# Splitting the second half's projection weights at fixed places in an attention loop

## The chip, the cores and the metric

The kernel runs on one core of a Trainium2 chip. A core has a matmul engine (TensorE, in the profile PE, with its weight loads as PEld), three engines for elementwise work (VectorE or DVE, ScalarE or ACT, GpSimd or POOL) and SyncE (SP), whose queue here issues every DMA. The metric is the device time of one execution in microseconds; lower is better. The kernel before takes 2299.53 us, the median of 2297.73, 2299.53 and 2301.41.

## The reference

One layer: causal linear attention with rotary positions over 4096 tokens of width 512 (16 query heads, 4 key/value heads, 128 wide), then a layer norm and a gated feed-forward part with Hadamard transforms. The change touches only the attention part:

```python
x: (1, 4096, 512)
q = (x @ Wq.T)   # 16 heads of 128
k = (x @ Wk.T)   # 4 heads of 128
v = (x @ Wv.T)   # 4 heads of 128
q = q * cos + rotate_half(q) * sin
k = k * cos + rotate_half(k) * sin
# each key/value head serves 4 query heads
qf = elu(q) + 1
kf = elu(k) + 1
# over tokens s, per head:
state = state + kf_s[:, None] * v_s[None, :]
z = z + kf_s
out_s = (qf_s @ state) / (qf_s @ z + EPS)
# then
out @ Wo.T
```

## The kernel before

**Products.** Every fp32 factor is held as two tiles, a rounded `hi` and the rest `lo`, and every product takes three matmuls (hi by hi, hi by lo, lo by hi). The pair is made by `hilo` (lines 94 to 99): ScalarE copies the source to `hi` (line 95) and VectorE or GpSimd, by its argument `eng`, subtracts to `lo` (line 96). A weight tile is 128x512. It is read from HBM into a *raw* tile and split from there into two tiles, `wh` and `wl`. Raw tiles come from the pool `praw`, with three buffers (line 64). The split weights live in the pool `wres`, with 28 buffers (line 63): 24 for the twelve tiles of one pass, and four more.

**Two passes, blocks and slots.** Attention runs in two passes over the tokens, s = 0 and s = 1, with half of the heads each: 8 query heads and 2 key/value heads, so that each pass needs twelve weight tiles of its own: two of v, two of k (one per key/value head g) and eight of q (four per g). A pass has 16 blocks of 256 tokens; blocks 16 to 31 are pass 1. A block has four *slots* `(n, g, p)`: a key/value head g and half p of the block's tokens (two chunks of 64). The loop over the 128 slots begins at line 534; slot i belongs to block i // 4, and pass 1 starts at slot 64.

**What a slot does.** `scores` forms the scores of two chunks (matmuls at lines 380 and 381, evacuation by ACT at 387, sums on DVE at 390 and 391, causal selects on POOL at 394). `av` multiplies scores and states into `ps_num` (line 414), which ACT empties at 418; `ps_num` has two PSUM buffers. `state` forms the chunks' states (337 to 354). Ahead of these go the projections for later slots: the q projection `proj_q(i + 5)` runs five slots ahead of its use (24 matmuls at line 288 into `ps_qk`, rotary steps at 268 to 278), `proj_k` and `proj_v` of the next block once per block (`proj_v` starts in slot (0, 1) with 24 matmuls at line 241 into `ps_v`, and sends its result through the DMAs `vs` and `vd`). `ps_qk` and `ps_v` share three PSUM buffers. So pass 1's v weights are first used in slot 61, its k weights in slot 60, and its q weights from slot 59 on, each with pass 0's work still going on.

**Weights of pass 1.** They go into the buffers that the same tiles of pass 0 and the spare four leave. In the loop's program `weights_v` and `weights_k` (198 to 203) stand at slot 54 (r = -6), `weights_q` (204 to 207) for the first key/value head at slot 56 (r = -4) and for the second at slot 58 (r = -2). Each loads a raw tile and splits it; the subtraction is on VectorE, for the odd q heads on GpSimd.

**The spare buffers.** `wcomb` (427 to 441) sums weights of the later feed-forward part on GpSimd, a step per slot: four tiles `wsum` of the pool `wres` are read, summed and stored to `was_d` in DRAM. It runs in slots 4 to 51 and 62 to 109.

**Order.** The program is traced in the order in which Python runs it, and a scheduler then orders each engine's queue (SP's DMA issues included) by readiness in its own model. An instruction that is *pinned* (`keep_in_program_order`, through `pin` and the argument of `dma`) keeps its place behind everything traced before it on its engine. The weight loads above are not pinned. Tiles of pools carry the dependencies: a tile's new writer waits until the old contents have been read.

Of the kernel before, what the change touches and what calls it, by code (L numbers as in the profile page):

```python
# [9 lines left out]
F32 = mybir.dt.float32  # L10
F32R = mybir.dt.float32r
# [12 lines left out]
QA = 5  # L24
# [19 lines left out]
def kernel(  # L44
# [6 lines left out]
    V, S, G, T = nc.vector, nc.scalar, nc.gpsimd, nc.tensor  # L51

    def dma(dst, src, pin=False):
        if dst.dtype == F32R:
            dst = dst.bitcast(F32)
        if src.dtype == F32R:
            src = src.bitcast(F32)
        i = nc.sync.dma_start(dst, src)
        if pin:
            tc.keep_in_program_order(i)  # L60

    cpool = ctx.enter_context(tc.tile_pool(name="cpool", bufs=1))
    wres = ctx.enter_context(tc.tile_pool(name="wres", bufs=28))
    praw = ctx.enter_context(tc.tile_pool(name="praw", bufs=3))
# [20 lines left out]
    def pin(i):  # L85
        tc.keep_in_program_order(i)
# [7 lines left out]
    def hilo(hi, lo, src, eng=V, pinned=False):  # L94
        i = S.activation(hi, src, AF.Copy)  # L95
        j = eng.tensor_tensor(lo, src, hi.bitcast(F32), ALU.subtract)  # L96
        if pinned:
            pin(i)
            pin(j)

    def load_w(src, pool=wres, eng=V, raw=None, **kw):
        raw = load_raw(src) if raw is None else raw
        hi, lo = (pool.tile([128, 512], F32R, tag="w", name=n, **kw) for n in ("wh", "wl"))
        hilo(hi, lo, raw, eng)
        return hi, lo

    WO = {}
    RAW0 = {}
# [3 lines left out]
    def wo_raw(h, raw):  # L112
        WR[h] = raw
        dma(raw, wo[h], True)
# [64 lines left out]
    with ExitStack() as es:  # L179
# [15 lines left out]
        W = {}  # L195
        blk = {}

        def weights_v(s, j):
            W["v", s, j] = load_w(wv[s, :, j * 512:(j + 1) * 512], raw=RAW0.pop(("v", s, j), None))

        def weights_k(s, g):
            W["k", s, g] = load_w(wk[2 * s + g], raw=RAW0.pop(("k", s, g), None))

        def weights_q(s, g):
            for h in range(4):
                W["q", s, g, h] = load_w(wq[8 * s + 4 * g + h], raw=RAW0.pop(("q", s, g, h), None),
                                         eng=G if h % 2 else V)
# [220 lines left out]
        def wcomb(p):  # L428
            r = {}
            for it in range(2):  # L430
                for kh in range(2):
                    x = wres.tile([128, 2, 2, 128], F32, tag="w", name="wsum")
                    dma(x, wug[2 * p + it].rearrange("p (u k m) -> p u k m", u=2, k=4)[:, :, 2 * kh:2 * kh + 2], True)
                    r[it, kh] = x
            yield
            yield
            for key, o, a, b, op in (("S3", (0, 0), (0, 0), (1, 0), ALU.subtract), ("S1", (1, 0), (1, 0), (1, 1), ALU.add),
                                     ("S2", (1, 1), (0, 0), (1, 1), ALU.subtract), ("S4", (0, 1), (0, 1), (1, 1), ALU.add)):
                pin(G.tensor_tensor(r[o], r[a], r[b], op))
                yield  # L440
                yield
                dma(was_d[p][key], r[o].rearrange("p u k m -> p (u k m)"), True)

        def wcomb_all():
            for p in range(8):
                yield from wcomb(p)
                yield
                yield
# [3 lines left out]
        def o_load(g, hi, lo):  # L452
            if g < 2:
                nt = praw.tile([128, 512], F32, tag="raw", name="nt0")
                dma(nt, num_d[0][:, g], True)
                rb = praw.tile([128, 512], F32, tag="raw", name="rb0")
                dma(rb, rec_d[0][g * 512:(g + 1) * 512].partition_broadcast(128), True)
            else:
                nt = ntx[:, g]
                dma(nt, num_d[0][:, g], True)  # L460
                pre_rb(g)
                rb = RB.pop(g)
            O0[g] = (hi, lo, nt, rb)

        def o_mul(g):
            pin(G.tensor_tensor(O0[g][3], O0[g][2], O0[g][3], ALU.mult))

        def o_split(g, eng):
            hi, lo, nt, rb = O0[g]
            hilo(hi, lo, rb.rearrange("p (h n) -> p h n", h=4), eng, True)  # L470
            cur.setdefault(0, {})[g] = (hi, lo)
# [32 lines left out]
        def go(gen):  # L504
            if gen is not None:
                next(gen, None)

        def run(gen):
            for _ in gen:
                pass  # L510
# [18 lines left out]
        for j in range(SA):  # L529
            run(scores(j))  # L530
        nsc = SA
        gw = wcomb_all()
        gk = gs1 = gv = None
        for i, (n, g, p) in enumerate(slots):
            nxt = n + 1 < N
            sl = (g, p)
            r = i - 4 * (NB - 1)
            if r == -6:
                for j in range(2):
                    weights_v(1, j)  # L540
                    weights_k(1, j)
            if r == 1 - QA:
                weights_q(1, 0)
            if r == 3 - QA:
                weights_q(1, 1)
            go(gq)
            if sl == (0, 1):
                go(gk)
# [44 lines left out]
            for x in gsc:  # L593
                go(x)
            gq = gq2
            if 4 <= i < 52 or 62 <= i < 110:
                go(gw)
            elif i == 113:
                o_load(0, *(wres.tile([128, 4, 128], F32R, tag="w", name=x) for x in ("oh0", "ol0")))
            elif i == 114:  # L600
                o_mul(0)
            elif i == 115:
                o_split(0, G)
                o_load(1, *(wres.tile([128, 4, 128], F32R, tag="w", name=x) for x in ("oh0", "ol0")))
            elif i == 116:
                o_mul(1)
            elif i == 117:
                o_split(1, G)
            elif i == 118:
                for h in range(3):  # L610
                    wo_raw(h, praw.tile([128, 512], F32, tag="raw", name="woraw"))
            elif i == 119:
                for x in ("xh", "xl"):
                    x = pe.tile([128, 4, 256], F32, tag=x, name="woraw").rearrange("p a b -> p (a b)")
                    wo_raw(len(WR), x[:, 0:512])
                    wo_raw(len(WR), x[:, 512:1024])
            elif i == 121:
                wo_split(G, 0, 1)
                wo_split(V, 2)
                for h in range(7, 10):  # L620
                    wo_raw(h, praw.tile([128, 512], F32, tag="raw", name="woraw"))
            elif i == 122:
                wo_split(G, 3, 4)
                wo_split(V, 5)
                o2 = [p3.tile([128, 2, 4, 128], F32R, tag=t, name=t, bufs=4) for t in ("qh", "ql")]
            elif i == 123:
                wo_split(G, 6)
                early.close()
                late["s"] = ExitStack()
                late["p"] = late["s"].enter_context(tc.tile_pool(name="cl", bufs=2, side="right", reuse_waits="tile"))  # L630
                ntx = late["p"].tile([128, 4, 512], F32, tag="nt", name="ntx", bufs=2)
                for y in range(2):
                    o_load(2 + y, o2[0][:, y], o2[1][:, y])
                x = p2.tile([128, 4, 512], F32, tag="vd", name="woraw")
                for h in range(10, 14):
                    wo_raw(h, x[:, h - 10])
                for h in range(14, 16):
                    wo_raw(h, ntx[:, h - 14])
                pre_rb(4)
                pre_yp(0)  # L640
                pre(1)
            elif i == 124:
                wo_split(G, 7)
                wo_split(V, 8)
            elif i == 125:
                o_mul(2)
                wo_split(G, 9)
                o_mul(3)
            elif i == 126:
                wo_split(G, 10)  # L650
# [135 lines left out]
    with ExitStack() as es:  # L786
# [100 lines left out]
        for t in range(32):  # L887
# [44 lines left out]
            if t >= 29 and t < 31:  # L932
                x = late["p"].tile([128, 16, 128], F32, tag="nt", name="araw0", bufs=2)
                x = x.rearrange("p (s u k) m -> p s u k m", s=4, u=2)
# [59 lines left out]
    with ExitStack() as es:  # L994
        pa = es.enter_context(tc.tile_pool(name="g1", bufs=1, reuse_waits="tile"))

        def utile(name):
            return pa.tile([128, 512], F32, tag="u", name=name, bufs=16)
# [19 lines left out]
        for n in range(NS):  # L1018
# [15 lines left out]
            for s, tag in enumerate(SEQ):  # L1034
                first = SEQ.index(tag) == s
                wh, wl = AOP.pop((n, s))
                yh, yl = YOPS[s]
                for u in (1, 0):
# [11 lines left out]
                    if s in (0, 2, 4):  # L1050
                        x = pa.tile([128, 512], F32, tag="sv", name="sv", bufs=6)
                        S.activation(x, ps, AF.Copy, scale=sc)  # L1052
                        sv[s, u] = x
                    if s in (1, 4, 6):
                        src, k, q = {1: (ps, 0, 0), 4: (bank.get(("b", u)), 4, 3), 6: (ps, 2, 1)}[s]
                        x = utile("cc")
                        V.scalar_tensor_tensor(x, src, sc, sv[k, u], ALU.mult, ALU.add)
                        emit(u, q, x)
                    if s == 5:
                        if u == 1:  # L1060
                            x = utile("sg")
                            S.activation(x, ps, AF.Silu, scale=sc)
                            c["g", 2] = x
                        else:
                            x = c.pop(("g", 2))
# [53 lines left out]
    with ExitStack() as es:  # L1119
# [38 lines left out]
        for idx, (n, s) in enumerate(order):  # L1158
# [19 lines left out]
            tag = SEQ[s]  # L1178
# [12 lines left out]
            for ip, j in ([(ip, j) for j in range(2) for ip in range(8)] if last else  # L1191
                          [(ip, j) for ip in range(8) for j in range(2)]):
                qd, r = divmod(ip, 2)
# [89 lines left out]
```

## Time and profile before

| | |
|---|---|
| three runs | 2297.73, 2299.53, 2301.41 us |
| profiled execution, its own time | 2299.27 us |
| its span, first to last instruction | 2297.6 us |
| mean granted TensorE clock | 0.994 |
| raw tile reads of the weights of pass 1 | first 376.18 us, last 446.36 us |
| their ACT copies (12) | 381.2 to 454.6 us, 0.63 us each |
| their DVE subtractions (8) | 381.8 to 454.3 us, median 0.69, up to 1.77 us |
| their POOL subtractions (4) | 438.2 to 455.3 us, median 1.35, up to 1.74 us |
| start of pass 1's first v projection | 450.05 us |

Matmuls are pipelined: a 128x256 one is recorded at 278 ns but the next starts some 115 ns later, so that short gaps do not appear as idle time, and the distance between two starts of the same step of the loop is the better ruler. The profile's times are those of one execution; the span and 1.67 us around it make its own time.

### The profile page before, as it was taken

Reading aid. Unit: us, or ns where it says so; the run is one execution under the profiler, and the core shown is the slowest. Engines: PE = TensorE matmul, PEld = TensorE weight load, DVE = VectorE, ACT = ScalarE, POOL = GpSimd, SP = SyncE. Lnnn points to the kernel's source line nnn. Section 1 sums busy time; section 2 is a strip of 40 time slices with the busy share of each in tenths; the row PEclk is TensorE's granted clock in tenths of the full one; section 3 lists DMA queues with packets and bytes.
Section 4 is the critical chain, followed back from the end, with each engine's and each line's share of the span. In section 5 each row is a group of like instructions: output and inputs, shape, how many; then the busy total and the mean of one; then the engine's idle time right before and its main releaser. Section 6 shows DMA issues by size and latency. Waiting matters only on the chain. (4 is left out here: it accounts for less than half of the span.)

```text
span 2297.6 us, 42221 instructions
## 1 busy us (share of the span) xinstructions
PE 2258.7 (98%) x14432; PEld 2004.3 (87%) x14432; DVE 1757.2 (76%) x2684; ACT 1393.8 (61%) x2515; POOL 1280.1 (56%) x1063
## 2 busy tenths in 40 slices
PE   8999999999999999899999999999999999999998
PEld 7999999899999998688878878878788888899998
DVE  8888888888888878688898775766766766675555
ACT  7777777777777767444443466665555655464553
POOL 5556666555555545568797535665555555633332
PEclk9999999999999999999999999999999999999999
DMA  6665665555555544889998976876765757887773
GB/s 195 176 181 167 184 181 171 168 156 150 167 165 154 170 135 142 301 271 277 284 285 258 309 252 214 253 239 190 230 208 186 242 185 211 260 276 238 227 251 121
DMA packets 369527, 484.15 MB, mean 211 GB/s; under 512 B 68670, under 2 KB 224384, under 8 KB 365344
## 3 DMA queue, kind: packets, MB, share of 16 engines
q1 hardware_dynamic: 369312, 481.45, 68.4%
q8 instruction: 114, 1.87, 0.3%
q14 instruction: 101, 0.83, 0.1%
HBM read 282.76 MB, written 156.76 MB: 191 GB/s over the span
## 5 line engine op out<-in xcount | busy, mean ns | idle before, releaser
L288 PE MATMUL ps_qk<-xh,wh 128*128 128x256 f32 x1280 | 355.3, 278 | 0.0
L288 PE MATMUL ps_qk<-xl,wh 128*128 128x256 f32 x1280 | 354.9, 277 | 0.0
L288 PE MATMUL ps_qk<-xh,wl 128*128 128x256 f32 x1280 | 354.4, 277 | 0.0
L394 POOL TENSOR_SCALAR_AFFINE_SELECT A<-A 64x512 fp32r<-64x512 f32 x256 | 211.5, 826 | 241.8 <-DVE am L390 145.0
L1027 POOL TENSOR_TENSOR cc<-cc 128x512 f32<-128x512 f32 x96 | 149.0, 1554 | 288.8 <-ACT cc L1024 109.7
L96 DVE TENSOR_TENSOR wol<-A,woh 128x512 fp32r<-128x512 f32 x217 | 223.3, 1036 | 104.4 <-ACT woh L95 92.7
L270 POOL TENSOR_TENSOR sw<-sw,csb 128x512 f32<-128x512 f32 x160 | 208.5, 1303 | 135.2 <-ACT sw L269 124.2
L288 PEld LDWEIGHTS ps_qk<-xh,wh 128*128 128x128 f32 x1280 | 240.7, 188 | 3.0
L288 PEld LDWEIGHTS ps_qk<-xh,wl 128*128 128x128 f32 x1280 | 240.4, 188 | 0.9
L288 PEld LDWEIGHTS ps_qk<-xl,wh 128*128 128x128 f32 x1280 | 240.6, 188 | 0.3
L95 ACT ACTIVATE woh<-A 128x512 fp32r<-128x512 f32 x217 | 135.5, 630 | 134.6 <-PE ps_b L1045 76.5
L95 ACT ACTIVATE hah<-hraw 128x512 fp32r<-128x512 f32 x216 | 133.7, 629 | 125.5 <-PE ps_da L1196 63.8
L96 POOL TENSOR_TENSOR hal<-hraw,hah 128x512 fp32r<-128x512 f32 x78 | 106.9, 1374 | 175.2 <-PE ps_da L1196 75.0
L1045 PE MATMUL ps_a<-yoh,woh 128*128 128x512 f32 x512 | 202.6, 397 | 1.2 <-ACT sv L1052 1.0
L1045 PE MATMUL ps_a<-yol,woh 128*128 128x512 f32 x512 | 202.4, 395 | 0.0
L1045 PE MATMUL ps_a<-yoh,wol 128*128 128x512 f32 x512 | 199.8, 396 | 0.0
L96 DVE TENSOR_TENSOR hal<-hraw,hah 128x512 fp32r<-128x512 f32 x138 | 108.7, 796 | 98.0 <-PE ps_da L1196 40.0
L1052 ACT ACTIVATE sv<-ps_a,wsc 128x512 f32<-128x512 f32 x192 | 127.0, 680 | 38.1 <-PE ps_a L1045 37.8
L173 PE MATMUL ps_wo<-wh,oh 128*128 128x512 f32 x372 | 147.8, 397 | 2.1 <-ACT oh L95 2.1
L173 PE MATMUL ps_wo<-wh,ol 128*128 128x512 f32 x372 | 147.6, 397 | 0.0
L173 PE MATMUL ps_wo<-wl,oh 128*128 128x512 f32 x372 | 147.3, 396 | 0.0
L271 DVE TENSOR_TENSOR ps_qk<-ps_qk,csb 128x512 f32<-128x512 f32 x160 | 111.2, 695 | 32.6 <-ACT sw L269 30.9
(280 smaller groups left out, 7356.4 us busy)
## 6 DMA issues: line engine op xcount, KB each, us to landing
hraw<-hop_d SPq DMA_DIRECT2D x224, 256.0 KB
vd<-vhl SPq DMA_DIRECT2D x128, 256.0 KB
num_d<-num SPq DMA_DIRECT2D x128, 256.0 KB
rb<-rec_d SPq DMA_DIRECT2D x128, 256.0 KB
hop_d<-hS SPq DMA_DIRECT2D x128, 256.0 KB
nt<-num_d SPq DMA_DIRECT2D x31, 1024.0 KB
A<-in_wug_dram SPq DMA_DIRECT2D x93, 256.0 KB
hop_d<-cc SPq DMA_DIRECT2D x64, 256.0 KB
```

The source lines that it names most:

```text
L95: i = S.activation(hi, src, AF.Copy)
L96: j = eng.tensor_tensor(lo, src, hi.bitcast(F32), ALU.subtract)
L173: T.matmul(ps, l[:, h], r, start=i == 0, stop=i == 47)
L270: G.tensor_tensor(sw, sw, sinb, ALU.mult)
L271: V.tensor_tensor(ps, ps, cosb, ALU.mult)
L288: T.matmul(ps[:, j], W[key][wa][:, k * 128:(k + 1) * 128], B[xa][:, k], start=i == 0, stop=i == 11)
L394: G.affine_select(ah, ah.bitcast(F32), pattern=[[0, 8], [1, 64]], compare_op=ALU.is_ge, fill=0.0, base=0, channel_multiplier=-1)
L1027: G.tensor_tensor(x, x, c.pop(("g", q)), ALU.mult)
L1045: T.matmul(ps, w[:, u, k], y[:, k], start=first and i == 0, stop=i == 5, skip_group_check=not first)
L1052: S.activation(x, ps, AF.Copy, scale=sc)
```

## The change

The three blocks of weight loads at the loop's head go. In their place a table `late_w` names, for five slots in a row (r = -4 to 0, that is slots 56 to 60), which weight tiles are split at the slot's end and on which engine: one tile of v; then the second of v and both of k; then three of q, three of q and two of q. The engines alternate, so that six subtractions are on VectorE and six on GpSimd. Copies and subtractions are pinned. At the end of the slot before, after that slot's own splits, the raw tiles are taken from `praw` and their DMAs are issued, pinned too (for slot 56 at the end of slot 55). The number of tiles and of buffers stays as it was, and so does `wcomb`. Lines below the second hunk stand ten further down.

```diff
+        late_w = {-4: [(("v", 1, 0), V)],
+                  -3: [(("v", 1, 1), G), (("k", 1, 0), V), (("k", 1, 1), G)],
+                  -2: [(("q", 1, 0, 0), V), (("q", 1, 0, 1), G), (("q", 1, 0, 2), V)],
+                  -1: [(("q", 1, 0, 3), G), (("q", 1, 1, 0), V), (("q", 1, 1, 1), G)],
+                  0: [(("q", 1, 1, 2), V), (("q", 1, 1, 3), G)]}
         gw = wcomb_all()
...
             r = i - 4 * (NB - 1)
-            if r == -6:
-                for j in range(2):
-                    weights_v(1, j)
-                    weights_k(1, j)
-            if r == 1 - QA:
-                weights_q(1, 0)
-            if r == 3 - QA:
-                weights_q(1, 1)
             go(gq)
...
             for x in gsc:
                 go(x)
             gq = gq2
+            if r in late_w:
+                for key, eng in late_w[r]:
+                    raw = RAW0.pop(key)
+                    hl = tuple(wres.tile([128, 512], F32R, tag="w", name=x) for x in ("wh", "wl"))
+                    hilo(*hl, raw, eng, True)
+                    W[key] = hl
+            if r + 1 in late_w:
+                for key, _ in late_w[r + 1]:
+                    raw = praw.tile([128, 512], F32, tag="raw", name="raw")
+                    src = {"v": lambda: wv[1, :, key[2] * 512:key[2] * 512 + 512], "k": lambda: wk[2 + key[2]],
+                           "q": lambda: wq[8 + 4 * key[2] + key[-1]]}[key[0]]()
+                    dma(raw, src, True)
+                    RAW0[key] = raw
             if 4 <= i < 52 or 62 <= i < 110:
                 go(gw)
```

## The prediction

> **What bounds the kernel.** First the page's section 1, for the engines' shares; then the busy table by stretches, for what a block of tokens costs undisturbed and in the stretch that the change touches; then the timeline, for each block's start; last the waits and the splits there.
>
> ```profile
> PE 2258.7 (98%) x14432; PEld 2004.3 (87%) x14432; DVE 1757.2 (76%) x2684; ACT 1393.8 (61%) x2515; POOL 1280.1 (56%) x1063
> ...
> 476.94:504.93 27.99, 27.99 (x229) 26.54 (x228) 23.11 (x39) 20.10 (x38) 13.92 (x15) 1.00 0.59 171
> 504.93:532.98 28.05, 28.05 (x230) 26.59 (x229) 24.10 (x39) 20.22 (x38) 15.69 (x17) 1.00 0.54 151
> ```
> (Stretch, length, busy PE, PEld, DVE, ACT, POOL, clock, DMA share, GB/s.) TensorE never rests in an undisturbed block, which takes 28.0 us, 7.0 per slot. Beside it lie 23.1 to 24.1 of DVE, 20.1 of ACT, 13.9 to 15.7 of POOL: per slot some 1.0 us of DVE, 2.0 of ACT and over 3 of POOL are free. Only what makes TensorE stop, or slows its clock, moves the end. The start of each block's v projection is the ruler:
>
> ```profile
> 360.50 0.39 PE L241 MATMUL ps_v<-wh,xh 128*128 128x256 f32 x1
> ...
> 450.05 0.28 PE L241 MATMUL ps_v<-wh,xh 128*128 128x256 f32 x1
> ...
> 504.93 0.39 PE L241 MATMUL ps_v<-wh,xh 128*128 128x256 f32 x1
> ```
> All splits of pass 1's weights (381 to 455 us) lie between 360.50 and 504.93: 144.43 us for five blocks. Five at 28.03 are 140.15. **4.3 us is all that this stretch loses, and so all that better placing can directly give back: 0.19%.** Where it goes:
>
> ```profile
> 400.00:410.00 10.00, 10.00 (x79) 9.19 (x78) 6.99 (x12) 6.18 (x12) 2.67 (x4) 1.00 0.95 271
> 410.00:420.00 10.00, 8.63 (x63) 7.58 (x63) 9.84 (x18) 6.54 (x11) 6.22 (x6) 1.00 0.30 89
> 440.00:450.00 10.00, 8.62 (x72) 8.03 (x71) 9.84 (x16) 8.58 (x15) 9.52 (x8) 1.00 0.46 141
> ```
> ```profile
> 403.80 0.77 SPq L58 DMA_DIRECT2D was_d3S<-wsum  x1
> 409.50 0.69 DVE L96 TENSOR_TENSOR wl<-raw,wh 128x512 fp32r<-128x512 f32 x1 [2.81 <-DMA was_d3S<-wsum]
> 440.79 1.77 DVE L96 TENSOR_TENSOR wl<-raw,wh 128x512 fp32r<-128x512 f32 x1
> ```
> At 409.50 DVE had stood 2.81 us in front of a split whose buffer was still being written out by a was_d store; it is full for the next 10 us (9.84) and TensorE loses 1.4. At 440 to 450 the q splits fill DVE (9.84) and POOL (9.52), and TensorE loses 1.4 again. The rest, 1.5 us, is scattered.
>
> **What the Trainium skill says.** "GPSIMD Engine Reference", section 1 (Specifications): GpSimd shares its SBUF interface with VectorE, and they contend. The trace agrees: a DVE split takes 0.69 us, 1.77 beside POOL's work at 440.79. "DMA: Bandwidth & Descriptors", "Issuing engines are not separate DMA queues": all transfers drain through the same sixteen engines and interleave. That store at 403.80 freed its reader after 5.7 us, and the raw tile issued at 376.18 was used at 381.17, 5.0 us later, both behind large stores. "TensorE: Matmul & The Clock Gate", Part 1, "What's actually happening": activity is judged in free-running windows of 3413 ns; after an idle one the clock is half. Here the trace shows that less than idleness is enough:
>
> ```profile
> 869.84:873.25 3.41, 1.61 (x7) 0.96 (x7) 3.32 (x6) 2.78 (x6) 1.76 (x2) 1.00 0.21 77
> 873.25:876.66 3.41, 3.40 (x16) 3.23 (x17) 3.41 (x7) 2.46 (x6) 3.32 (x3) 0.50 0.00 0
> 446.58:450.00 3.42, 2.04 (x15) 1.53 (x14) 3.36 (x6) 2.86 (x6) 3.26 (x4) 1.00 0.45 154
> ```
> A window with TensorE busy 1.61 us was followed by one at clock 0.50; one with 2.04 busy was not. I take 1.8 us of standing in one window as the point; each half-speed window costs 1.7 us.
>
> **The change, part by part.**
>
> *Count.* Twelve splits before and after: 12 ACT copies of 0.63 us as before, 6 instead of 8 subtractions on DVE (2 x 0.69 = 1.4 us less), 6 instead of 4 on POOL (2 x 1.35 = 2.7 more). With TensorE the bound that alone is worth nothing: both engines have room in an average slot.
>
> *Removed.* No split stands at slot 54 or 55, when was_d stores are fresh. The sums that own those buffers stop at slot 51, four slots (28 us) ahead of the first split at the end of slot 56, against 5.7 us for a store. The 2.81 us wait and its 1.4 us go, and so do the 1.4 at 440 to 450 with the scattered 1.5: -4.3 at most. Late next is what follows.
>
> *Moved.* The q weights of slot 64's projection, which TensorE reaches five slots ahead, are split at the ends of slots 58 and 59, pinned behind all traced work, where the old code asked for them from the start of slot 56. The order of the built program shows the result: at slot 59 only 2 of the 24 matmuls of that projection follow the scores, then 11 num matmuls, 12 more that need the DVE halves, 2 of the next projection, and the 10 that need POOL's half. Weights now set TensorE's order for slots 58 to 62; before, the projection ran in one piece.
>
> *The reads.* There are three raw buffers and waves of one, three, three, three and two tiles; a wave is issued when the splits of the wave before are done with their buffers. For the end of slot 58 SP issues the tiles behind the v block's vs and vd copies:
>
> ```profile
> 508.69 1.64 SPq L58 DMA_DIRECT2D vs<-v  x2
> 510.96 3.35 SPq L58 DMA_DIRECT2D vd<-vhl  x4
> ```
> That is the next block's pattern: the last vd leaves SP at 514.31, 9.4 us after its v projection started (504.93). Plus about 5 us from issue to use, the first q tile is usable 14 us after the v projection of block 15. Behind a pinned ACT copy that waits for it stand ACT's evacuations of scores and num, so DVE's score sums, POOL's selects and TensorE's num wait too. Walking the four queues in the built order with the trace's durations (ACT 0.6, DVE 0.69, POOL split 1.35, sine product 1.3, select 0.65 to 1.04), from that v projection: ACT idle from 11 to 14, TensorE stands 1.4 us at 10 (scores behind the sums of the scores before), 1.0 at 13.7 (the first q weight); then the held-up copies come together: from 14 to 33 ACT has 23 copies of the slots themselves and the 6 splits of two waves, 29 of 0.62 us, 18 of 19 us. There are two num buffers in PSUM; the third num after the stall finds ACT still behind with the first, and TensorE waits 2.0 to 2.5 us at about 31, and 0.4 to 0.8 for scores just after. 1.4 + 1.0 + 2.2 + 0.6 = 5.2 us. Bounds: 0, if reads land in 2 us less and ACT never falls behind; 8, if DVE's operations beside POOL's take the 1.1 to 1.8 us seen at 440.79 instead of 0.69. I take 6.5, in the upper half, because the walk has no contention and POOL has 2.7 us more.
>
> *The clock.* 2.4 us of standing within one window is above the point; 1.4 + 1.0 within 4.7 us may be. One or two windows at half speed: 1.7 to 3.4 us, more likely than not given those stalls; I take 3.0.
>
> *Later.* In the built order, apart from this stretch, a few transposes and copies swap places at 930 to 1120 us, where TensorE had lost 1.35 and 0.9 us once each. Nothing there is new work: 0, within ±2. A moved window phase can also take away or add a half-speed window at 873 or 914, ±3.4.
>
> **Sum:** 2299.27 (span 2297.6 and 1.67 around it) - 4.3 + 6.5 + 3.0 = 2304.5; the profiled run lies 0.26 below the median of the runs, which makes **2304.8 us**, +0.23%.
>
> **The rivals.**
> *One loss for another.* The late weights cost the walk's 5.2 us with no half-speed window: 2299.5 - 4.3 + 5.2 = 2300.4. For it: 446.58 to 450.00 stood 1.4 us without a clock drop. Against: the longest stall at slot 61 is above the point.
> *The stalls vanish.* ACT and DVE keep to the average block (2.0 and 1.0 us free per slot against 1.9 and 0.7 to 1.4 asked), the reads land early: -4.3 gives 2295.2, with a swap in the later stage or a half-speed window gone (1.7) 2293.5. For it: the loads by slot just fit, and the splits are spread over five slots where the old lay in two clumps. Against: the tiles come 14 us into the block, as worked out. It decides if the first q tile is usable at 11 us or sooner.
> *It does not do what it says.* The scheduler may place the old splits anyhow; but the new ones are pinned, and the built order shows them in their slots. I give it nothing of its own.
>
> **How the numbers follow.** 0.2%, 4.6 us, is about what this kernel's measurement tells from no change. Chances: late weights with the clock drop (2302 to 2312) 0.53; one loss for another 0.32; stalls vanish 0.15. Nearly all of the first is slower by over 0.2% (0.47 with 0.06 just inside), of the second a little (0.03) is too; of the third about 0.12 is faster, if something of the later stage comes with it. So faster 0.12, same 0.38, slower 0.50. Range 2294.5 to 2311: up to the first case's bound of 8 plus two windows and the later ripple, down to the third with half of its chance.
>
> **What would show it.** Right: the v projections of blocks 15 and 16 lie over 29.5 us apart; no was_d wait ahead of a wl; waits of ACT wh on raw tiles; PE waits on num and wh between; a window below full clock there. Wrong: five blocks in about 140 us; or the time differs by more than the stretch does, which would put it in the stage after attention.

## The result

The changed kernel is slower: 2308.1 us (median of six runs, 2305.76 to 2310.88) against 2299.39 (six runs of the kernel before, 2297.73 to 2301.41), a ratio of 1.0035, 95% interval [1.0026, 1.0045]. Run again later, beside the kernel before, it gave 1.0035 [1.0021, 1.0049]. The profiled execution took 2305.76 us, its span is 2304.0.

The page's shares hardly move: two DVE instructions fewer, two POOL instructions more, TensorE as before the bound.

```profile
PE 2261.4 (98%) x14432; PEld 2007.7 (87%) x14432; DVE 1762.1 (76%) x2682; ACT 1393.4 (60%) x2515; POOL 1286.2 (56%) x1065
```

The ruler, the starts of the v projections in TensorE's timeline of the changed kernel (start, duration):

```profile
359.75 0.38 PE L241 MATMUL ps_v<-wh,xh 128*128 128x256 f32 x1
387.82 0.39 PE L241 MATMUL ps_v<-wh,xh 128*128 128x256 f32 x1
415.87 0.38 PE L241 MATMUL ps_v<-wh,xh 128*128 128x256 f32 x1
445.63 0.28 PE L241 MATMUL ps_v<-wh,xh 128*128 128x256 f32 x1
482.47 0.41 PE L241 MATMUL ps_v<-wh,xh 128*128 128x256 f32 x1
510.17 0.38 PE L241 MATMUL ps_v<-wh,xh 128*128 128x256 f32 x1
```

(The v projection at 445.63 belongs to block 15, the last of pass 0; its counterpart before is the one at 450.05. The first v projection of pass 1 is the one at 482.47, before at 476.94, and not at 450.05 as the table of the kernel before has it.)

The first two blocks are now undisturbed (28.07 and 28.05 us; they took 29.46 and 28.65). Most of the loss shows in the block from 445.63, which takes 36.84. Single blocks are not cut at the same work, though: counted by their starts, the last three hold 237, 235 and 212 matmuls, an undisturbed one 228 (the tables also count those that run over an edge). The five together hold 1140 in every kernel of this document, so their sum is the fair ruler. Five blocks take 150.42 us against 144.43: +5.99, while the spans differ by 6.4. So nearly all of the profiled loss lies in the stretch that the change touches, and there between 444 and 486 us. The table by stretches of the changed kernel (length, busy PE, PEld, DVE, ACT, POOL, clock, DMA share, GB/s) shows it in two parts:

```profile
445.63:482.47 36.84, 32.11 (x237) 29.68 (x236) 29.75 (x46) 26.54 (x50) 23.57 (x24) 0.91 0.54 168
...
455.39:458.80 3.41, 1.86 (x10) 1.37 (x10) 2.40 (x5) 0.69 (x1) 0.89 (x2) 1.00 1.09 247
458.80:462.21 3.41, 3.34 (x15) 2.85 (x15) 2.54 (x6) 3.15 (x6) 1.70 (x3) 0.50 1.05 372
475.87:479.28 3.41, 1.51 (x13) 1.17 (x11) 2.47 (x4) 3.35 (x7) 3.41 (x3) 1.00 0.01 2
479.28:482.69 3.41, 2.25 (x9) 1.96 (x10) 3.35 (x7) 2.06 (x6) 2.59 (x4) 0.50 0.21 78
482.69:486.11 3.42, 3.42 (x18) 3.42 (x18) 3.39 (x9) 1.83 (x6) 0.94 (x1) 0.50 0.03 5
```

TensorE stands in two clusters, and behind each the clock is halved: for one window after the first and for two after the second, where TensorE stands again in the first of the two. Three windows of 3.41 us at 0.50 cost at most 5.1 us; the kernel before had none between 360 and 510. Counting the excess over an undisturbed 140.2 us, 150.42 is 10.2 of excess: 5.1 of clock and 5.1 of standing. (In the window at 479.28 TensorE is busy for only 2.25 us, so that half speed costs some 1.1 there and not 1.7; by this estimate it is 4.5 of clock and 5.7 of standing.) The kernel before had 4.2, all standing. **The change exchanged 4.2 us of standing for a little over 5, and then paid about 5 for a clock that fell.**

What TensorE stood for, in its list of waits from 440 to 500 us (waiting instruction, what released it, us in total, times, longest):

```profile
PE ps_sc L380 <- DVE A L391: 2.6, 2, 1.6
PE ps_num L414 <- ACT num L418: 2.0, 1, 2.0
PE ps_num L414 <- POOL A L394: 0.5, 1, 0.5
```

And where this comes from, in the timeline of SP and of ACT:

```profile
451.12 3.38 SPq L58 DMA_DIRECT2D vd<-vhl  x4
454.60 2.09 SPq L58 DMA_DIRECT2D raw<-in_wq_dram  x3
```
```profile
455.78 0.69 ACT L275 ACTIVATE sw<-ps_qk,neg 128x512 f32<-128x512 f32 x1 [1.48 <-DVE ps_qk L274]
459.01 0.63 ACT L95 ACTIVATE wh<-raw 128x512 fp32r<-128x512 f32 x1 [2.54 <-DMA raw<-in_wq_dram]
459.55 0.61 ACT L353 ACTIVATE sh<-s 128x512 fp32r<-128x512 f32 x1
```

The first q tiles are read at 454.60, directly behind the four vd copies, and the first is usable at 459.01, 13.4 us into the block. ACT stands 2.54 us in front of it, with a copy of state behind it in its queue.

### The profile page after: what moved, and what is told of

The parts are those of the page before. It is cut to its first block, busy times and chain, and to the rows that moved or that the text cites. A ratio compares the mean times of both kernels' runs of the same rounds, so it can differ in the third digit from the quotient of the medians.

```text
span 2304.0 us, 42203 instructions
## 1 busy us (share of the span) xinstructions
PE 2261.4 (98%) x14432; PEld 2007.7 (87%) x14432; DVE 1762.1 (76%) x2682; ACT 1393.4 (60%) x2515; POOL 1286.2 (56%) x1065
```

## The experiments

The theory to be tested was that the q weights come too late for TensorE: read late behind the vd copies, split late because the v and k tiles come first. Rivals: three splits in one slot are too many wherever they stand; two subtractions on GpSimd in one wave delay the scores; the pins as such.

One table for all. "Five blocks" and "half-speed" are of the profiled execution between 360 and 515 us; "standing" is five blocks less 140.2 and less 1.7 per half-speed window, and so a little too small where TensorE also stands within such a window; the mean clock is that of all its timed runs, and the kernel before had 0.9944 or 0.9945 in each of the three groups of experiments. A profile is one execution of many, so the ratio decides.

| kernel | ratio, 95% interval | five blocks | half-speed windows | standing | mean clock |
|---|---|---|---|---|---|
| before | 1 | 144.43 | 0 | 4.2 | 0.9944 |
| changed | 1.0035 [1.0026, 1.0045] | 150.42 | 3 | 5.1 | 0.9922 |
| changed, again | 1.0035 [1.0021, 1.0049] | 150.65 | 3 | 5.3 | 0.9924 |
| all one slot earlier | 1.0020 [1.0012, 1.0029] | 147.38 | 1 | 5.5 | 0.9934 |
| first q wave read early | 1.0006 [0.9997, 1.0014] | 146.98 | 1 | 5.1 | 0.9938 |
| engines as before | 1.0029 [1.0020, 1.0037] | 146.94 | 1 | 5.0 | 0.9933 |
| not pinned | 1.0021 [1.0015, 1.0028] | 148.23 | 2 | 4.6 | 0.9936 |
| by need | 0.9987 [0.9981, 0.9994] | 142.50 | 0 | 2.3 | 0.9948 |
| by need and spread | 1.0028 [1.0021, 1.0035] | 149.88 | 2 | 6.3 | 0.9930 |
| no loads | 0.9985 [0.9978, 0.9993] | 140.19 | 0 | 0 | 0.9945 |
| before, sums early | 1.0003 [0.9996, 1.0010] | 145.48 | 1 | 3.6 | 0.9939 |
| waves swapped | 1.0015 [1.0009, 1.0022] | 147.27 | 1 | 5.4 | 0.9936 |

**All one slot earlier.**

```diff
-            r = i - 4 * (NB - 1)
+            r = i - 4 * (NB - 1) + 1
```

> The changed kernel with its whole table one slot earlier (reads from the end of slot 54, splits at the ends of slots 55 to 59). Theory (the q weights come a slot too late for TensorE, and their reads stand behind block 15's vd copies): the waits of ACT on raw q tiles (2.5 us at 459) and TensorE's wait on num (2.0 us at 479) go, no half-speed window between 360 and 515, and five blocks from the v projection at 360 take 141 to 143 us against 150.4; time 2296 to 2299, a ratio of 0.9985 to 1.000 to the kernel before. Rival (three splits pinned in one slot overfill ACT and POOL wherever they stand): five blocks stay at 147 us or more, time 2304 or more.

By its figures this is the rival's case: 147.38 us and 2304.34. It takes 0.15% off the changed kernel, but does not reach the kernel before. That does not yet speak for the rival, because q tiles are still late. The first three q tiles now come before the vd copies, and the next wave falls behind them in their place: its reads are issued at 458.15, behind vd copies from 452.82 to 456.2, ACT stands 1.97 us at 460.85 for them, and TensorE stands 0.9 us for that weight:

```profile
452.82 3.40 SPq L58 DMA_DIRECT2D vd<-vhl  x4
458.15 1.30 SPq L58 DMA_DIRECT2D raw<-in_wq_dram  x3
```
```profile
460.85 0.63 ACT L95 ACTIVATE wh<-raw 128x512 fp32r<-128x512 f32 x1 [1.97 <-DMA raw<-in_wq_dram]
```

A uniform shift changes which q tile is late; one still is. Of the standing that is left, 1.1 us for num and 2.4 for scores, up to 478.45, lie around the start of the half-speed window; this run does not trace them to a tile.

**First q wave read early.** Only the reads of the three tiles move, a slot ahead, into free weight buffers; the splits stay.

```diff
+            if r == -4:
+                for key, _ in late_w[-2]:
+                    raw = wres.tile([128, 512], F32, tag="w", name="raw")
+                    dma(raw, wq[8 + 4 * key[2] + key[-1]], True)
+                    RAW0[key] = raw
-            if r + 1 in late_w:
+            if r + 1 in late_w and r != -3:
```

> The changed kernel, with only the three q tiles of the first q wave read a slot earlier (end of slot 56, into free weight buffers, ahead of block 15's v copies); all splits where the change puts them. If the late read is what counts: ACT's 2.5 us wait on raw q goes, TensorE's stalls at 459 (0.5) and 479 to 481 (2.0 and 1.0) shrink below 1 us together, five blocks take 144 to 147 us, time about 2302. If it is the place of the pinned splits that counts: TensorE still stands over 2.5 us at 476 to 482, five blocks take 148 to 151, time 2305 to 2308.

By the ratio the late read is the larger part: 0.29% comes off (1.0035 to 1.0006, some 6.7 us), and the median, 2302.03, is what the first branch said. ACT no longer waits for a q tile, and TensorE's wait for ACT to empty num is gone from its list. But the stalls do not shrink as that branch said: the profiled execution still shows 5.1 us of standing, now for scores and selects (1.4 us up to 459, then 1.6 and 0.5 up to 480). At 2305.45 us in all it was the slowest of this kernel's runs, so its stretch may not be typical. The mean clock rises from 0.9922 to 0.9938, which alone is 3.7 us of 2305. One more thing moves with the edit: the three raw buffers stay free for the second q wave, whose reads are issued together at 458.89 (in the changed kernel two at 460.39 and the next at 464.30). So the gain is not that of the first wave's reads alone.

**Engines as before.** The second wave's two subtractions on GpSimd go to VectorE (8 and 4).

```diff
-                  -3: [(("v", 1, 1), G), (("k", 1, 0), V), (("k", 1, 1), G)],
+                  -3: [(("v", 1, 1), V), (("k", 1, 0), V), (("k", 1, 1), V)],
```

> The changed kernel with the subtractions of the second wave (v, k, k) all on VectorE, as before the change; so 8 on VectorE and 4 on GpSimd. If GpSimd's two subtractions in that wave delay the sine product and so the scores: TensorE's 1.6 us wait on scores at 456.9 goes with the half-speed window after it (1.7), five blocks take about 147 us, time about 2304.5. If the late read alone matters: the stall stays and so does the time, 2307 to 2309.

Its interval overlaps that of the changed kernel: no gain that can be told, and the time is that of the second branch. TensorE's wait for scores, up to 457.8, is still 1.2 us (1.6 in the changed kernel). The profile alone would have misled: it caught the fastest of 13 runs (2300.91; their median is 2307.47).

**Not pinned.** The same places in the program, `pinned` left out of the splits and reads.

```diff
-                    hilo(*hl, raw, eng, True)
+                    hilo(*hl, raw, eng)
...
-                    dma(raw, src, True)
+                    dma(raw, src)
```

> The changed kernel with splits and reads at the same places of the program but not pinned, so that the scheduler may move them ahead. If the pins are the cost: five blocks take 141 to 145 us, time 2296 to 2300. If the place in the program is: the scheduler cannot move them far (three raw buffers), five blocks take 147 or more, time 2304 or more.

This is the second branch, 148.23 us and 2304.74, though not for its reason: the scheduler does move the splits ahead (the first copy is at 382.18 us, 440.63 in the changed kernel). The losses are spread over three blocks, two half-speed windows remain, and 0.14% comes off. So the pins are a small part of the cost at most.

**By need.** The experiment that decides. Same slots, same counts, same engine at each position; only the tiles change places, in the order in which TensorE asks for them.

```diff
-        late_w = {-4: [(("v", 1, 0), V)],
-                  -3: [(("v", 1, 1), G), (("k", 1, 0), V), (("k", 1, 1), G)],
-                  -2: [(("q", 1, 0, 0), V), (("q", 1, 0, 1), G), (("q", 1, 0, 2), V)],
-                  -1: [(("q", 1, 0, 3), G), (("q", 1, 1, 0), V), (("q", 1, 1, 1), G)],
+        late_w = {-4: [(("q", 1, 0, 0), V)],
+                  -3: [(("q", 1, 0, 1), G), (("q", 1, 0, 2), V), (("q", 1, 0, 3), G)],
+                  -2: [(("k", 1, 0), V), (("k", 1, 1), G), (("q", 1, 1, 0), V)],
+                  -1: [(("q", 1, 1, 1), G), (("v", 1, 0), V), (("v", 1, 1), G)],
```

> The changed kernel with the same slots, the same number of splits in each and the same alternation of engines, but the tiles in the order in which TensorE needs them (q of the first head, k, q, v, q). Theory A (what costs is that q tiles come after TensorE wants them): the waits on wh and num go, five blocks take 141 to 143.5 us, time within 0.05% of the kernel before. Theory B (what costs is three splits in one slot on VectorE, GpSimd and ACT, whichever tile): TensorE still loses 4 to 6 us by standing, now as waits on scores behind VectorE, five blocks 145.5 to 150 us, ratio 1.001 to 1.003.

2296.83 us: by the ratios 0.48% below the changed kernel, and 0.13% below the kernel before, with an interval under 1 (0.9987 [0.9981, 0.9994]). Theory A was right on the stretch, and too cautious on the time. There is no half-speed window in the stretch. The load on each engine and each slot is what the changed kernel has, so three splits in one slot aren't by themselves what costs. ACT even waits as long for raw tiles (1.34 and 1.66 us, 3.0 in all, as in the changed kernel), but the first of these waits is for a k tile, read behind the vd copies in the place where the change had q:

```profile
460.06 0.63 ACT L95 ACTIVATE wh<-raw 128x512 fp32r<-128x512 f32 x1 [1.34 <-DMA raw<-in_wk_dram]
```

TensorE meanwhile runs the q projection without a wait, eight matmuls in a row and the others in turn with scores and num. Here is its start in TensorE's timeline, where the changed kernel could run two matmuls of it at 459.69 and then turned to the num matmuls:

```profile
458.94 0.28 PE L288 MATMUL ps_qk<-xh,wh 128*128 128x256 f32 x1
459.05 0.29 PE L288 MATMUL ps_qk<-xl,wh 128*128 128x256 f32 x1
459.18 0.28 PE L288 MATMUL ps_qk<-xh,wl 128*128 128x256 f32 x1
```

What is left is one wait of 1.6 us, of the v projection for a PSUM buffer that VectorE frees:

```profile
PE ps_v L241 <- DVE ql L368: 1.6, 1, 1.6
PE ps_num L414 <- POOL A L394: 0.5, 1, 0.5
```

The profiled execution, 2294.07 us, is the fastest of its 20 runs, but the mean clock of all 20, 0.9948, is no lower than that of the kernel before. Of the some 11 us between the medians of the changed kernel and this one, the profiles place 7.9 in the stretch (150.42 against 142.50); where the rest lies these runs do not show.

**By need and spread.** By need, in slots 54 to 60, one subtraction per engine and slot at most.

```diff
+        late_w = {-6: [(("q", 1, 0, 0), V)],
+                  -5: [(("q", 1, 0, 1), G), (("q", 1, 0, 2), V)],
+                  -4: [(("q", 1, 0, 3), G), (("k", 1, 0), V)],
+                  -3: [(("k", 1, 1), G), (("q", 1, 1, 0), V)],
+                  -2: [(("q", 1, 1, 1), G), (("v", 1, 0), V)],
+                  -1: [(("v", 1, 1), G), (("q", 1, 1, 2), V)],
+                  0: [(("q", 1, 1, 3), G)]}
```

> By need, and spread over seven slots (54 to 60) with at most one subtraction on VectorE and one on GpSimd in a slot. Theory A: as by need, 141 to 143.5 us. Theory B: clearly less than by need, TensorE stands 1 to 3 us in all, no window at half speed, five blocks 141.5 to 143.5; ratio 0.9985 to 0.9998, faster than the kernel before.

A clear miss: both theories expected it to be at least as good, and it is 0.41% slower than by need alone. ACT's timeline and SP's point to the reason. The first tile is read at 428.88, behind the vd copies of block 14, and ACT stands 3.99 us in front of it; behind block 15's vd copies it stands 2.69 more:

```profile
423.34 3.38 SPq L58 DMA_DIRECT2D vd<-vhl  x4
428.88 0.36 SPq L58 DMA_DIRECT2D raw<-in_wq_dram  x1
```
```profile
433.10 0.63 ACT L95 ACTIVATE wh<-raw 128x512 fp32r<-128x512 f32 x1 [3.99 <-DMA raw<-in_wq_dram]
```

When the tile of a pinned copy is late, what stands behind the copy in ACT's queue waits with it. ACT stands 7.3 us for raw tiles here, 3.0 by need. TensorE's longest wait, 2.0 us for a state copy of ACT, ends at 447.69. That these holds cause it is read from the order of events; no run takes them away alone. As it stands, both seem to matter: that the tile TensorE needs next isn't late, and that ACT isn't held for long. Even splits per slot did not make up for that.

**No loads.** The control.

```diff
+            if r == -6:
+                for k in [k for k in W if k[1] == 0]:
+                    W[(k[0], 1) + k[2:]] = W[k]
```

> A control: pass 1's weights are neither read nor split; pass 1 takes the tiles of pass 0 (its results are those of the wrong heads). Both theories: five blocks 140.2 us, no half-speed window between 360 and 515; the time is what a perfect placing would give, 2295 to 2296.5, ratio 0.998. If the ratio is above 0.999, standing in this stretch isn't what the time hangs on, and the rest of the run gives the gain back.

140.19 us for the five blocks, as the ruler said, no half-speed window, and by the ratio 0.15% off the time (3.4 us where 4.3 were there to be had); the median, 2297.23, lies a little above what was expected. This is the ceiling of any placement in this stretch. By its ratio, by need reaches it within the measurement, though its profile keeps 2.3 us of standing.

**The kernel before, sums early.**

```diff
-            if 4 <= i < 52 or 62 <= i < 110:
+            if 2 <= i < 50 or 62 <= i < 110:
```

> The kernel before, with the weight sums of the later stage two slots earlier (slots 2 to 49 in place of 4 to 51), so that no was_d store is fresh when its splits start. If that wait cost what the prediction says: VectorE's 2.8 us wait goes, five blocks 142.5 us in place of 144.4, time 1.5 to 2 us less. If the wait only hides another: VectorE waits for something else there and five blocks stay at 144 or more.

The wait for the was_d store is gone, and nothing is gained. TensorE now stands 2.7 us in one piece, up to 448.81, for ACT to empty a num buffer, and the clock is halved from 448.36 on for one window:

```profile
PE ps_num L414 <- ACT num L418: 2.7, 1, 2.7
PE ps_num L414 <- ACT sh L353: 0.8, 1, 0.8
```

**Waves swapped, and the changed kernel again.** The first q wave a slot earlier, in exchange with the second v tile and k.

```diff
-                  -3: [(("v", 1, 1), G), (("k", 1, 0), V), (("k", 1, 1), G)],
-                  -2: [(("q", 1, 0, 0), V), (("q", 1, 0, 1), G), (("q", 1, 0, 2), V)],
+                  -3: [(("q", 1, 0, 0), G), (("q", 1, 0, 1), V), (("q", 1, 0, 2), G)],
+                  -2: [(("v", 1, 1), V), (("k", 1, 0), G), (("k", 1, 1), V)],
```

> The changed kernel with its second and third wave exchanged: the first three q tiles are split at the end of slot 57 and the second v tile with both k tiles at the end of slot 58; counts, engines by position and the other waves stay. If it is the first q wave's lateness alone that costs (theory A in its narrow form): no half-speed window between 440 and 490, five blocks 142 to 144 us, ratio to the kernel before 0.998 to 0.9997. If the later q tiles (end of slots 59 and 60) are as late for TensorE as the first: at least one stall over 1.8 us stays at 470 to 482, five blocks 145 to 148, ratio 1.0005 to 1.0025.

> The changed kernel once more, beside the waves swapped and the kernel before on the same chip: 1.0026 to 1.0045 times the kernel before, 145 to 151 us for the five blocks, mean clock 0.992 to 0.993 where the kernel before has 0.9944. If the half-speed windows of the first profile were chance, the mean clock is that of the kernel before and the ratio 1.000 to 1.001.

Swapping the waves brings less than half of what by need brings. The waits up to 457 and 459 go (one of 1.0 us, up to 462, comes in), but a stall of 2.7 us up to 477.52 remains (num behind ACT), and a half-speed window after it. The narrow form falls. Three things differ from by need: the first q tile is split at the end of slot 57 (by need at 56), the fourth q tile and the first of the second head are still split at the end of slot 59 (by need at 57 and 58), and ACT stands 2.5 us for the v tile that is now read behind the vd copies. Which of the three makes the stall these runs do not separate. The changed kernel, run again, shows the same three windows and nearly the same standing, and its five runs the same low clock: the windows are no chance of one profile.

## Why the prediction was right

2304.8 us was forecast, 2308.1 measured, inside the range and in the likeliest case (2302 to 2312). By its steps:

- *The ruler* held: 140.15 was said for five undisturbed blocks, the control without loads took 140.19.
- *Removed.* No split waits for a was_d store any more, and the blocks from 360 and 388 run clean, as said. But the sums-early experiment shows that the wait for the store, taken away alone, brings nothing; the prediction gave it 1.4 us. TensorE stood for longer further on, up to 448.81.
- *The reads.* vd's last issue 9.4 us into the block and the first tile usable at 14 were forecast; 454.50 - 445.63 = 8.9 and 459.01 - 445.63 = 13.4 were measured. ACT idle from 11 to 14: idle from 10.8 to 13.4.
- *The walk.* Forecast from the start of the block: 1.4 us for scores at 10, 1.0 for the q weight at 13.7, 2.0 to 2.5 for num at 31, 0.4 to 0.8 for scores after it. Measured: 1.6 for scores, ending at 11.3; about 0.5 for the weight at 14.1 (an estimate: the list of waits does not have it, and in the changed kernel run again has 0.4); 2.0 for num, ending at 33.8; 1.0 for scores, ending at 35.8. With the 0.5 at 444 these waits make 5.6, and by the ruler the standing is 5.1 (5.7 by the estimate above); the walk said 5.2. The 6.5 that the sum took, to allow for contention beside GpSimd, was too much by the ruler; slower operations there were (POOL splits of 1.69 and 1.73 us ahead of the first stall), but moving them to VectorE brought nothing that can be told.
- *The path to the wait for num* was right only in part. The walk had ACT behind all the way from 14 to 33. In the trace ACT had caught up in between and stood for a projection:

```profile
465.55 0.59 ACT L268 ACTIVATE sw<-ps_qk 64x512 f32<-64x512 f32 x1 [1.95 <-PE ps_qk L288]
```

It runs without a gap only from 471.73 to the num copy at 478.79, with two splits and the first rotary steps of three projections in between. So what came together were, as far as the trace shows, the projections that had stood back for their weights, more than the copies held up at 459. That the size and the place came out so near is in part luck.
- *The clock* is the mis-sized term: one or two windows, 3.0 us, were forecast, and three came, at most 5.1 us. The second cluster reaches into the next window, and two windows were slow. Over all runs the mean clock gives the same size: 0.9922 against 0.9944 is 0.0022 x 2305 = 5.1 us of the 8 that the ratio makes. Standing taken 1.4 too large and the clock 2.1 too small offset each other in part, so that the total came nearer than its parts.
- *Later.* Forecast 0 within 2. In the profiled pair the time after the stretch is 1793.8 us against 1792.7, some 1.2 more.

The sum from the parts as measured is 2299.4 - 4.2 + 5.1 + 5.1 = 2305.4, which is near the profiled run (2305.76). The other runs of the changed kernel lie above it, and of the 2.3 us from there to the median some may be further half-speed windows and swaps in the later stages; no run here isolates them, so that stays open.

The Trainium skill, "TensorE: Matmul & The Clock Gate", Part 1, "What's actually happening", speaks of idle windows of 3413 ns. The windows here fit in length (3.41 us), but they need not be idle, and the measurement decides: just ahead of a slow window TensorE was busy for 1.86 and 1.51 us in the stretch of the changed kernel, and for 1.22 with the waves swapped. Nor is the prediction's point of 1.8 us of standing sharp. The kernel before had a window with 2.69 us busy ahead of a slow one, which the prediction did not use, and by need had one with 1.84 after which the clock stayed:

```profile
471.46:474.88 3.42, 1.84 (x16) 1.67 (x15) 3.39 (x7) 3.23 (x8) 2.27 (x3) 1.00 0.54 158
474.88:478.29 3.41, 3.41 (x31) 3.39 (x30) 3.35 (x6) 2.48 (x6) 3.04 (x3) 1.00 0.04 8
```
```profile
910.80:914.21 3.41, 2.69 (x16) 2.00 (x16) 3.05 (x5) 3.41 (x9) 3.25 (x4) 1.00 0.21 78
914.21:917.62 3.41, 3.41 (x16) 2.60 (x14) 3.32 (x6) 2.78 (x7) 3.25 (x4) 0.50 0.43 154
917.62:921.03 3.41, 3.41 (x15) 2.79 (x15) 2.24 (x5) 1.92 (x4) 2.97 (x4) 0.50 0.56 155
```

(The first fence is of by need, the second of the kernel before.) Counted over the windows of all twelve traces, from 60 to 2285 us: of those at full speed, all 30 in which TensorE was busy for up to 1.51 us were followed by half speed, 26 of 120 with more, up to 2.7 us, and none of the 7600 above that. What decides in between these runs do not show, nor why in the kernel before the clock stayed low after 914.21, where TensorE is recorded as busy throughout.

## What to carry to other kernels

When work is placed by hand, order it by when the bound engine asks for each piece, before asking how many pieces fit in a slot: with the same load per slot, the order alone was worth 0.48% here (of which 0.13% is gain over the kernel before). Follow each read from its place in the DMA queue: the first q read stood behind 3.38 us of copies in SP's queue, and the pinned copy that waited for it held ACT for 2.54 us. And add to every stall the clock that it may cost: 4.2 us of standing cost 4.2 where the clock held, a little over 5 in two clumps cost 10.2.

## What had not been expected

- Spreading the splits evenly made the kernel slower than leaving them in waves (1.0028 against 0.9987), with waits of 3.99 and 2.69 us of ACT for single late tiles.
- A wait of 2.81 us of VectorE, in full view ahead of a TensorE stall, could be removed without any gain (1.0003 [0.9996, 1.0010]).
- Behind two stalls of 2.0 and 1.0 us, one microsecond apart, the clock was halved for 6.8 us, which cost up to 3.4, about as much again as the stalls.
